# The MLP of the first eight tiles moved into the second batch pair's attention, and the stretch behind it put in a modelled order

## The chip, the cores and the metric

The kernel runs on one core of one Trainium2 chip, in one launch. A core has five engines that are programmed apart: TensorE (PE; its weight loads are listed apart as PEld), VectorE (DVE), ScalarE (ACT), GpSimd (POOL) and SyncE (SP), the last of which here only issues DMAs. Each engine runs its own queue of instructions in order and waits on semaphores for the others. The metric is the time of one execution on the device in microseconds (us), and less is better.

## What is computed

Input is x with B, T, C = 4, 1024, 128 in float32, and the output has the same shape. Four blocks follow one another, each on the layer norm of what came before:

```python
x = x + attention(layernorm(x))     # 16 heads of 8; a row sees its last 32 rows and every 64th one before it
x = x + ffn(layernorm(x))           # h = [x, -x]; weights +1 or -1
x = x + mamba(layernorm(x))
x = x + ffn(layernorm(x))           # the same weights

def ffn(x):                                          # k0 256x512, k1 512x512, k2 512x128: bool
    h = s0 * (concat([x, -x]) @ where(k0, 1., -1.))
    h = s1 * ((relu(h) * 2) @ where(k1, 1., -1.))
    return s2 * ((relu(h) * 2) @ where(k2, 1., -1.))

def mamba(x):                                        # E = 256 channels, N = 16 states
    u, z = split(layernorm_gb(x) @ W_in)             # 128 -> 2 x 256
    u2 = silu(conv4(u) + conv_b)                     # depthwise, causal, 4 taps
    dt_lo, Bm, Cm = split(u2 @ W_xp)
    dt = softplus(dt_lo @ W_dt + b_dt)
    h[t] = exp(dt[t] * A) * h[t-1] + dt[t] * u2[t] * Bm[t]   # per channel and state
    y = (sum over states of h * Cm) + u2 * D_param
    return x + res_scale * ((y * silu(z)) @ W_out)
```

## The kernel before

All work on the four compute engines is issued through a thin wrapper (`InOrder`, L49 to L60). While the list `keep` is not empty, each instruction is pinned to its place in program order, so that within its engine nothing overtakes; where the list is empty, the build's scheduler may move instructions by its own priorities. Since the call that records every instruction is L57, nearly all rows of the profile have that line, and the tiles' names tell them apart.

**Data.** The rows are held in two buffers `xs[0]` and `xs[1]`, one for each pair of batches (bp). A tile is 128 rows: 64 of each batch of the pair. A pair has 16 tiles, and a chunk (bp, c) is four tiles, 512 columns once turned. The notation "(0,2)" below is chunk 2 of pair 0. For Mamba a part (b, f) is one half (f) of one batch (b).

**Stage 1, attention (L201 to about L591).** A software pipeline of turns, one tile each: 32 tiles, with seven turns ahead (`LEAD`, L541) and five behind. In turn i the stages of several tiles are issued one after the other, in the order that is written out in the loop (L546 on): POOL's `strided_products` of tile i-1 (prodv) and `product` of i+1 (prod); PE's `weights` of i-2 (pt, four transposes); on DVE `scores_before`, `divide` of i-4, `strided` of i-2 (or), `weights_own` (eo); ACT copies pt into ep and POOL subtracts eo from it (`weights_before`); PE's output projection of i-5 (py) and DVE's residual; PE's `scores` of i+1 (ps), which ACT copies into S; DVE's `softmax_scores` (the strided sums, the row maximum mx, the subtraction) and ACT's two exponentials (E); PE's `turn_out` (po) and `values` (pa). Each tile of a pair has one more strided row block than the one before, so prod, prodv, or and S grow within a pair. Between these stages two steps of `prep_steps` (L274 to L349) of a later chunk are issued: the normalised rows xn, their transposes tp and xnT, the projections pq, pk and pn, the loads that spread the keys into kx (L330) and the values into vd, vr (L342, L345). `spread_values` (L477) copies vr into the value blocks on ACT, one quarter a turn in turns 4c-1 to 4c+2 of its chunk. PSUM has eight banks of 2 KB for each partition: ps has two, mx one, and five in turn serve all else (`spare`, L213). `stats` and `scales` (L244, L254) make the norm's factors (sta and mva on DVE, rsa on POOL). At turn 0 SP loads the MLP's weights as bytes (`load_mlp`, L106).

**Between attention and scans (L648 to L1237).** DVE turns the bytes into float32 weights w0, w1 and w2, in buffers that a pool frees again (L648 to L675). Mamba's weights are loaded on SP and POOL's queues (L792 to L835), among them `taps`, 512 KB, from which w_conv is made. The MLP (`mlp`, L682) takes one chunk: statistics (st_f, mv_f, rs_f), normalised rows (fxn), transposes (ftp, fxnT), the first layer (pf to h1), the second (pg to h2: 64 matmuls of 512 columns for a chunk, in two groups of 32), the third (pfo), and the residual. Each activation is held as a high and a low half in a format called f32r, so w0 and w1 are applied twice, while w2 is applied in float32. Names have an a behind them for the first MLP and b or c for the one at the end (pga, pgb, pgc). In the first batch pair's case the statistics (L244's kind, in the trace st_fa, mv_fa, rs_fa) are placed by the scheduler as soon as rows are ready.

Such a function is a generator of `Piece`s: a few instructions with a rough cost for each engine and the PSUM banks that they take. A `Work` (L598 to L645) is a stream of them. Two lanes of work hold the MLP chunks: lane 0 has (0,0), (0,2), (1,0), (1,2) of the first MLP, then chunks of the last one; lane 1 the odd ones. For the first scan part two more works run beside them: `mamba_norm` (L848: statistics, factors rs_z, rows mxn, transposes, the norm that becomes x itself, mxnT) of chunks (0,0) and (0,1), and `mamba_pre_half` (L903: pc, the four taps as matmuls; px; pd; dt; du). The loop at L1216 to L1237 gives each of the works one piece in turn, but the lanes none while `mamba_pre_half` has a PE piece next, until du of the first part is there. `keep` is empty here.

**Scans (L1044).** 128 units, one for each of 8 parts and 16 states: db (POOL), da (ACT), the scan hs (DVE), pcc (PE), hc (DVE), their sum (POOL) and pys (PE). Within a unit, `evictions` and `pieces` (L1155, L1165) issue pieces of the other works, by budgets for each engine (`RATES`, L1144) and three spare banks (`SPARE`, L1142). `ready` (L1185) forces what a part needs. At the end of the scans what is left of the works is issued, and then (L1255 on) the last batch's output (pmo_own) and its MLP (pfc, pgc, pfoc).

Of the kernel before, what the change touches and what calls it, by code (L numbers as in the profile page):

```python
# [16 lines left out]
F32 = mybir.dt.float32  # L17
BF16 = mybir.dt.bfloat16
I32 = mybir.dt.int32
U8 = mybir.dt.uint8  # L20
# [6 lines left out]
P = 128  # L27
# [16 lines left out]
def hybrid_kernel(ctx: ExitStack, tc: tile.TileContext, x, Wq, Wk, Wv, Wo, ln_g, ln_b, W_in, conv_w,  # L44
# [56 lines left out]
    k0s = const.tile([P, 2, FF], U8, name="k0s")  # L101
    k1s = const.tile([P, 4, FF], U8, name="k1s")
    k2s = const.tile([P, 4, C], U8, name="k2s")
    scal = const.tile([P, 4], F32, name="scal")

    def load_mlp():  # L106
        for t, k in ((k0s, k0), (k1s, k1), (k2s, k2)):
            nc.sync.dma_start(t, k.rearrange("(i p) f -> p i f", p=P))
        for i, s in enumerate((s0, s1, s2, res_scale)):
            nc.sync.dma_start(scal[:, i : i + 1], s.partition_broadcast(P))  # L110
# [88 lines left out]


    def attention(actx):  # L201
# [8 lines left out]
        pr = actx.enter_context(tc.tile_pool(name="attpr", bufs=5, space=PSUM))  # L210
# [63 lines left out]
        def prep_steps(cc):  # L274
# [3 lines left out]
            xn = ap2.tile([P, 4, C], F32, name=f"xn{cc}", tag="xn")  # L278
# [11 lines left out]
            xnT = ap2.tile([P, CH], F32, name=f"xnT{cc}", tag="xnT")  # L290
# [33 lines left out]
            else:  # L324
                kT = ap2.tile([P, CH], F32, name=f"kT{cc}", tag="kT")
# [17 lines left out]
            vr = ap2.tile([P, 16, C], F32, name=f"vr{cc}", tag="vr")  # L343
# [7 lines left out]
        S, E, prods, prodv, ew, psum, outs = ({} for _ in range(7))  # L351
# [54 lines left out]
        def softmax_scores(i):  # L406
# [9 lines left out]
            mx = pw.tile([P, H], F32, name=f"mx{i}", tag="mx")  # L416
# [119 lines left out]
        def residual(i):  # L536
            bp, m = tiles[i]
            ve.tensor_add(xs[bp][:, m, :], xs[bp][:, m, :], psum.pop(("y", i))[:, :C])
# [3 lines left out]

        starts = {(3 if cc == 1 else 4 * cc) - LEAD: cc for cc in range(len(tiles) // 4)}
        preps = []
        last = len(tiles)
        for i in range(-LEAD, last + 5):  # L546
# [6 lines left out]
            if i == 0:  # L553
                load_mlp()
# [14 lines left out]
            if i >= 0:  # L569
                at(1, scores)  # L570
                at(1, keep_scores)
            at(0, softmax_scores)
            at(0, softmax_exp)
# [5 lines left out]
            at(-3, values)  # L579
            at(-4, keep_out)  # L580
# [7 lines left out]
            cc, step = divmod(i + 1, 4)  # L588
            if 0 <= cc < last // 4:
                spread_values(cc, range(step, step + 1))  # L590
# [57 lines left out]
    fw = ctx.enter_context(tc.tile_pool(name="ffnw", bufs=1))  # L648
    fx = ctx.enter_context(tc.tile_pool(name="ffnx", bufs=2))
    with tc.tile_pool(name="kload", bufs=1) as kl:  # L650


        sign = fw.tile([P, 2], F32, name="sign")
        below = fw.tile([P, 2], F32, name="below")
        ve.tensor_single_scalar(sign, scal[:, 0:2], 0.0, op=ALU.is_gt)
        ve.tensor_single_scalar(below, scal[:, 0:2], 0.0, op=ALU.is_lt)
        ve.tensor_sub(sign, sign, below)
        total = fw.tile([P, 1], F32, name="total")
        ve.tensor_mul(below, scal[:, 0:2], sign)
        ve.tensor_scalar_mul(below, below, 2.0)  # L660
        ve.tensor_mul(total, below[:, 0:1], below[:, 1:2])
        ve.tensor_mul(total, total, scal[:, 2:3])
        twice = fw.tile([P, 2], F32, name="twice")
        ve.tensor_scalar_mul(twice, sign, 2.0)

        w0 = fw.tile([P, FF], F32R, name="w0")
        diff = kl.tile([P, FF], F32, name="diff")
        ve.tensor_sub(diff, k0s[:, 0], k0s[:, 1])
        ve.tensor_scalar_mul(w0, diff, twice[:, 0:1])
        w1 = fw.tile([P, 4, FF], F32R, name="w1")  # L670
        ve.tensor_scalar(w1, k1s, twice[:, 1:2], sign[:, 1:2], ALU.mult, ALU.subtract)
        w2 = fw.tile([P, 4, C], F32R, name="w2")
        ve.tensor_scalar(w2, k2s, 2.0, -1.0, ALU.mult, ALU.add)
    waste = fw.tile([P, C], F32, name="waste")
    fed = set()  # L675
# [121 lines left out]
    def vec(name, src, n):  # L797
        t = mw.tile([P, n], F32, name=name)
        nc.gpsimd.dma_start(t, src.rearrange("(h p) -> p h", p=P))
        return t  # L800

    g_t, b_t = vec("ln_g", ln_g, 1), vec("ln_b", ln_b, 1)
    cb_t, bdt_t, dp_t = vec("cb", conv_b, NH), vec("bdt", b_dt, NH), vec("dp", D_param, NH)
    w_in = mw.tile([P, 2 * E], F32, name="w_in")
    nc.sync.dma_start(w_in, W_in)

    w_xp = mw.tile([P, NH, 6 * N + DR], F32, name="w_xp")
    xp = W_xp.rearrange("(h p) r -> p h r", p=P)
    for i in range(3):
        nc.gpsimd.dma_start(w_xp[:, :, 2 * N * i : 2 * N * (i + 1)], xp[:, :, DR:])  # L810
    nc.gpsimd.dma_start(w_xp[:, :, 6 * N :], xp[:, :, :DR])
    w_dt = mw.tile([6 * N + DR, E], F32, name="w_dt")
    nc.gpsimd.dma_start(w_dt[6 * N :, :], W_dt)
    a_t = mw.tile([P, NH, N], F32, name="a_t")
    nc.gpsimd.dma_start(a_t, A_log.rearrange("(h p) n -> p h n", p=P))
    sc.activation(a_t, a_t, AF.Exp)
    ve.tensor_scalar_mul(a_t, a_t, -1.0)
    w_out = mw.tile([P, NH, C], F32, name="w_out")
    nc.sync.dma_start(w_out, W_out.rearrange("(h p) c -> p h c", p=P))
    gp.tensor_scalar_mul(w_out, w_out, scal[:, 3:4])  # L820

    w_conv = mw.tile([P, DC, E], F32, name="w_conv")
# [375 lines left out]
    def in_scan_buffers(u):  # L1198

        return [m2.tile([P, 2, CH], F32R, name=f"h1{u}_{f}", tag="hc", bufs=6) for f in range(4)]  # L1200
# [89 lines left out]
```

## Time and profile before

| | |
|---|---|
| median of 3 runs | 929.82 us (927.71 to 930.09) |
| profiled execution, its own time | 926.49 us |
| span of the profiled execution | 924.7 us |
| PE busy | 759.3 us (82%), 5642 matmuls |
| DVE busy | 756.4 us (82%), 1013 instructions |
| ACT busy | 592.4 us (64%), 1299 instructions |
| POOL busy | 747.9 us (81%), 586 instructions |
| mean granted clock of PE | 0.896 of full |
| DMA | 53.09 MB, mean 57 GB/s |
| chain that ended last | DVE 30%, PE 26%, POOL 17%, ACT 14%, issue 8% |
| 0 to 136.6 us: busy PE, DVE, ACT, POOL | 100.43, 113.45, 75.59, 116.77 us |
| 240.1 to 248.5 us: busy PE; clock | 5.05 us; 0.58 |

The profile is of one execution. Busy is the sum of the durations of an engine's instructions; the chain follows the last instruction back to what released it, step by step. A stretch is given as start and end from the span's start. A row "out<-in" names the tile that an instruction writes and those that it reads; "<-POOL prodv" behind an idle time names what ended it.

### The profile page before, as it was taken

The page shows a single profiled execution, that of the slowest core. Times are in us where ns is not written, and L with a number is a line of the kernel's source. Part 1 is how long each engine was busy: PE and PEld are TensorE (multiplying, and loading weights), DVE is VectorE, ACT ScalarE, POOL GpSimd, SP SyncE. Part 2 cuts the span into 40 slices and gives each one's busy share as a digit, 9 for nine tenths or more (in the row PEclk, how much of TensorE's full clock was granted, in tenths as well). Part 3 has the DMA queues.
Part 4 walks back from the last instruction along what each step waited for, and adds up shares of the span by engine and source line. Part 5 has one row for each costly group of instructions (what it writes and reads, how often), then busy time and mean ns, then how long its engine had stood idle before and what let it go on. Part 6 is the DMA issues. An engine that isn't in the chain of part 4 may idle for free.

```text
span 924.7 us, 15264 instructions
## 1 busy us (share of the span) xinstructions
PE 759.3 (82%) x5642; PEld 455.5 (49%) x5642; DVE 756.4 (82%) x1013; ACT 592.4 (64%) x1299; POOL 747.9 (81%) x586
## 2 busy tenths in 40 slices
PE   5797768865788979897789798869889798888887
PEld 2455435543466534542356444425446355554566
DVE  6699898999633278889799888898998999999842
ACT  4775537743345577889867767876878765655413
POOL 6699996999533188999989988999989999989621
PEclk9899769997599979897999989968989899898998
DMA  4633123330100111121111122121121212121000
GB/s 122 128 71 70 41 37 68 73 65 2 42 7 1 47 69 50 45 67 70 68 58 58 46 68 71 45 70 46 69 82 62 86 50 78 69 80 58 24 23 12
DMA packets 47162, 53.09 MB, mean 57 GB/s; under 512 B 4824, under 2 KB 38400, under 8 KB 47088
## 3 DMA queue, kind: packets, MB, share of 16 engines
q1 hardware_dynamic: 45920, 51.59, 19.7%
q8 instruction: 44, 0.72, 0.3%
q0 software_dynamic: 608, 0.27, 0.2%
q10 hardware_dynamic: 560, 0.26, 0.1%
q14 instruction: 30, 0.25, 0.1%
HBM read 45.82 MB, written 4.46 MB: 54 GB/s over the span
## 4 chain that ended last, share of the span: by engine, by line
DVE 30%; PE 26%; POOL 17%; ACT 14%; issue 8%; SPq 3%; DMA 1%; DVEq 0%; POOLq 0%; ACTq 0%
DVE hs L57 14%; DVE hc L57 4%; PE pga L57 4%; PE pys L57 4%; POOL db L57 4%; POOL prod L57 3%; DVE S L57 3%; ACT da L57 3%; POOL prodv L57 3%; PE pgb L57 2%; PE pc L57 2%; SPq L330 2%; ACT L57 2%; POOL hc L57 2%; PE pfoa L57 2%
## 5 line engine op out<-in xcount | busy, mean ns | idle before, releaser
L57 POOL TENSOR_TENSOR db<-du,bs 128x1024 f32<-128x1024 f32 x128 | 302.5, 2364 | 0.4 <-DMA bs<-bd 0.4
L57 ACT ACTIVATE da<-dt,a_t 128x512 f32<-128x512 f32 x256 | 175.4, 687 | 126.7 <-DVE hs L57 126.3
L57 POOL TENSOR_TENSOR hc<-hc,hc 128x512 f32<-128x512 f32 x128 | 163.0, 1274 | 43.7 <-DVE hc L57 43.6
L57 DVE TENSOR_TENSOR hc<-hs,pcc 128x1024 f32<-128x1024 f32 x128 | 156.0, 1219 | 28.6 <-PE pcc L57 21.1
L57 DVE TENSOR_TENSOR_SCAN hs<-da,db 128x512 f32<-128x512 f32 x128 | 149.4, 1207 | 14.3 <-ACT da L57 14.1
L57 DVE TENSOR_TENSOR_SCAN hs<-da,carry,db 128x512 f32<-128x512 f32 x128 | 157.1, 1267 | 4.5 <-ACT da L57 4.5
L57 PE MATMUL pys<-hc,ident 128*128 128x512 f32 x256 | 146.0, 655 | 0.8 <-POOL hc L57 0.8
L57 PE MATMUL pcc<-bc,spread 96*128 96x512 bf16 x128 | 52.8, 413 | 34.8 <-DVE hc L57 33.8
L57 PE MATMUL pga<-h1a,w 128*128 128x512 f32 x256 | 73.9, 439 | 3.1 <-ACT gate L57 2.2
L57 PEld LDWEIGHTS pys<-hc,ident 128*128 128x128 f32 x256 | 51.0, 209 | 51.2 <-issue 31.8
L57 POOL TENSOR_TENSOR prodv<-vS,E 128x128 f32<-128x128 f32 (+14 forms) x30 | 69.3, 2311 | 5.8 <-ACT E L57 5.6
L57 POOL TENSOR_TENSOR prod<-kv,qs 128x128 f32<-128x128 f32 (+14 forms) x30 | 71.1, 2369 | 1.5 <-DVE or L57 1.4
L57 PE MATMUL pc<-mxnT,w_conv 128*128 128x512 f32 x128 | 61.7, 608 | 5.9 <-ACT gate L57 5.9
L57 PEld LDWEIGHTS pga<-h1a,w 128*128 128x128 f32 x256 | 51.2, 202 | 27.6 <-issue 7.3
L57 ACT ACT_TABLE_LOAD x48 | 61.6, 1283 | 3.4 <-issue 2.6
L57 PE MATMUL pgb<-h1b,w 128*128 128x512 f32 x192 | 58.9, 453 | 4.4 <-DVE fxnTc L57 3.1
L57 ACT ACTIVATE E<-S 128x512 f32<-128x512 f32 (+15 forms) x62 | 26.5, 473 | 52.3 <-DVE S L57 52.1
L57 PE MATMUL ps<-kx,qT 64*32 64x256 f32 x1008 | 47.8, 448 | 6.3 <-DVE S L57 5.4
L57 PEld LDWEIGHTS pgb<-h1b,w 128*128 128x128 f32 x192 | 38.0, 199 | 26.7 <-issue 7.8
L57 PE MATMUL py<-woT,oT 128*128 128x128 f32 x64 | 18.0, 368 | 40.0 <-ACT oT L57 39.8
L57 POOL TENSOR_TENSOR ep<-ep,eo 128x512 f32<-128x512 f32 x32 | 40.9, 1278 | 9.9 <-ACT ep L57 8.7
L57 ACT COPY ep<-pt 128x512 f32<-128x512 f32 x32 | 18.7, 586 | 38.4 <-DVE eo L57 36.5
(217 smaller groups left out, 1560.9 us busy)
## 6 DMA issues: line engine op xcount, KB each, us to landing
bs<-bd SPq DMA_DIRECT2D x64, 512.0 KB
vr<-vd SPq DMA_DIRECT2D x32, 256.0 KB
vd<-kv SPq DMA_DIRECT2D x8, 256.0 KB
x<-in_L_attn_a_x_dram SPq DMA_DIRECT2D x15, 128.0 KB
kx<-kT SPq DMA_DIRECT2D x104, 16.0 KB
out_dram<-x SPq DMA_DIRECT2D x12, 128.0 KB
taps<-in_L_attn_b_conv_w_dram SPq DMA_DIRECT2D x1, 512.0 KB
k1s<-in_L_ffn_k_dram SPq DMA_DIRECT2D x1, 256.0 KB
```

Source lines behind the costliest of these rows:

```text
L57: ins = getattr(self.engine, name)(*args, **kwargs)
L330: queues[h % len(queues)].dma_start(kx[rows, :, h % HB, :], kT[rows, :].rearrange("p (t x) -> p t x", t=4))
```

## The change

1. **Weights and loads.** The MLP's bytes have no buffers of their own any more. At turn 15 they are loaded into the attention buffer of pair 0's keys and values (tag "kv"), which is free then, and turns 16 to 19 make w0, w2 and w1 of them on DVE. Mamba's loads (`load_mamba`, now 11 on SP and none on POOL) are issued at turn 8; taps, w_dt and w_out come after the attention. w_conv, spread, minus_i and the scaling of w_out are pieces of a work of their own (`tables_between`).
2. **MLP of tiles 0 to 7.** It runs in the second pair's turns (17 to 33), in pairs of tiles, 256 columns: `first_te` issues one of four PE steps a turn (transposes and the third layer of the pair before; 8 matmuls of the first layer; two steps of 16 of the second), `first_sc` and `first_ve` empty its banks one turn later. Statistics stand in turns 15 and 16, and those of the following norm in turns 33 and 34. The lanes begin with (0,2) and (0,3), and `mamba_norm` takes the ready factors.
3. **PSUM.** Six banks in place of five serve the attention's `spare`; mx has none of its own, and is put into columns 128 to 143 of the bank that py of five tiles before has used.
4. **Other buffers.** xn, xnT, kT and vr have one buffer in place of two. The loads of vr are issued two turns later, `spread_values` copies two quarters a turn in turns 4c+1 and 4c+2, and chunk 1's preparation starts a turn later.
5. **Order between attention and scans.** It is pinned, and made by a small model: each engine has a time from which it is free, each work one from which its next piece can start, and the piece with the earliest start is next; lanes get a malus of 1.0 us, and may hold at most five banks together with the others.

The diff, cut to its core:

```diff
-    def load_mlp():
-        for t, k in ((k0s, k0), (k1s, k1), (k2s, k2)):
-            nc.sync.dma_start(t, k.rearrange("(i p) f -> p i f", p=P))
+    def load_scales():
...
+    def mlp_weights(k0s, k1s, k2s):
...
+        ve.tensor_scalar_mul(twice, sign, 2.0)
+        yield
+        ve.tensor_sub(w0, k0s[:, 0], k0s[:, 1])
+        ve.tensor_scalar_mul(w0, w0.bitcast(F32), twice[:, 0:1])
+        ve.tensor_scalar(w2, k2s, 2.0, -1.0, ALU.mult, ALU.add)
+        for i in range(2):
+            yield
+            part = slice(2 * i, 2 * i + 2)
+            ve.tensor_scalar(w1[:, part], k1s[:, part], twice[:, 1:2], sign[:, 1:2], ALU.mult, ALU.subtract)
...
-        pr = actx.enter_context(tc.tile_pool(name="attpr", bufs=5, space=PSUM))
+        pr = actx.enter_context(tc.tile_pool(name="attpr", bufs=6, space=PSUM))
...
-            mx = pw.tile([P, H], F32, name=f"mx{i}", tag="mx")
+            mx = (left_over.pop(i) if i in left_over else spare(f"mx{i}"))[:, C : C + H]
...
-            ve.tensor_add(xs[bp][:, m, :], xs[bp][:, m, :], psum.pop(("y", i))[:, :C])
+            left_over[i + 5] = py = psum.pop(("y", i))
+            ve.tensor_add(xs[bp][:, m, :], xs[bp][:, m, :], py[:, :C])
...
+        def first_te(k):
+            p, step = divmod(k, 4)
+            h1, xnT, h2, xn = (first[n] for n in ("h1", "xnT", "h2", "xn"))
+            if step == 0:
+                if p:
+                    po = first["po"] = spare(f"mo{k}")[:, :cols]
+                    for t in range(2):
+                        for f in range(4):
+                            te.matmul(
+                                po[:, t * C : (t + 1) * C], h2[:, f, t * C : (t + 1) * C], w2[:, f].bitcast(F32),
+                                start=f == 0, stop=f == 3,
+                            )
+                if 2 * p < FIRST:
+                    tp = first["tp"] = spare(f"mt{k}")[:, :cols]
+                    for t in range(2):
+                        te.transpose(tp[:, t * C : (t + 1) * C], xn[:, t * C : (t + 1) * C], ident)
+            elif step == 1:
...
+                            te.matmul(
+                                pf[:, f], w0[:, (f0 + f) * P : (f0 + f + 1) * P], xnT[:, s], start=s == 0, stop=s == 1
+                            )
+            else:
+                f0 = 2 * step - 4
+                pg = first["pg"] = spare(f"mg{k}").rearrange("p (f c) -> p f c", f=2)
+                for f in range(2):
+                    for j in range(4):
+                        for s in range(2):
+                            te.matmul(
+                                pg[:, f], w1[:, j, (f0 + f) * P : (f0 + f + 1) * P], h1[:, j, s],
+                                start=j + s == 0, stop=j == 3 and s == 1,
+                            )
...
+            if i == NT // 2:
+                load_mamba()
+            if i == NT - 2:
+                finish_mamba()
+            if i == NT - 1:
+                first_rooms()
+                weights_made = mlp_weights(*first["codes"])
+            step = i - NT - 1
+            if step == 0:
+                first_norm(0)
+            if 0 < step <= STEPS:
+                first_sc(step - 1)
             at(-1, strided_products)
...
             if i >= 0:
                 at(1, scores)
                 at(1, keep_scores)
+            if 0 < step <= STEPS:
+                first_ve(step - 1)
+            if NT <= i < NT + 4:
+                next(weights_made, None)
             at(0, softmax_scores)
+            if NT - 1 <= i <= NT:
+                first_stats(range(4 * (i - NT + 1), 4 * (i - NT + 2)), "mv")
+            c = i - NT - STEPS
+            if 0 <= c < 2:
+                first_stats(range(4 * c, 4 * c + 4), "after")
             at(0, softmax_exp)
...
             at(-3, values)
+            if 0 <= step < STEPS:
+                first_te(step)
             at(-4, keep_out)
...
-            early(0, lane, f1, lane, *[in_scan_buffers] * lane),
             early(0, 2 + lane, f1, lane),
...
-            wanted = first[-1].may() and "pe" in first[-1].next.us
-            for w in first + ([] if wanted else lanes):
-                if w.may():
-                    w.run()
+            able = []
+            for w in first + lanes:
+                if not w.may() or (w in lanes and w.next.banks and w.held + w.next.banks + sum(v.held for v in first) > 5):
+                    blocked.add(w)
+                    continue
...
+                start = max([since[w], *(free[k] for k in w.next.us)])
+                able.append((start + (1.0 if w in lanes else 0.0), len(able), start, w))
+            start, w = min(able)[2:]
+            us = w.next.us
+            w.run()
+            end = start + sum(us.values()) + (0.1 if us else 0.0)
+            since[w] = end
+            for k in us:
+                free[k] = end
```

## The prediction, made before the changed kernel ran

> **What bounds the kernel now.** I read four views of the profile, in this order. First the busy time by stage, with stage borders that I took from the timeline: 136.6 us is where the second batch's first turn starts, 240.1 the end of its last full turn, 248.5 the last residual of the attention, 324.6 the first scan (hs), 885.9 the end of the last one. The columns are the stage, its length, busy time of PE, PEld, DVE, ACT and POOL, the granted clock of PE, the DMA share and GB/s.
>
> ```profile
> 136.60:187.10 50.50, 45.63 (x971) 29.41 (x969) 46.39 (x101) 37.30 (x99) 41.69 (x39) 0.98 0.34 67
> 187.10:240.10 53.00, 31.73 (x777) 22.24 (x776) 49.48 (x71) 19.18 (x46) 53.00 (x21) 0.77 0.15 29
> 248.50:324.60 76.10, 67.48 (x294) 48.39 (x295) 27.62 (x68) 43.03 (x86) 22.27 (x34) 0.91 0.10 29
> 324.60:885.90 561.30, 478.92 (x1700) 267.01 (x1699) 506.64 (x493) 406.56 (x845) 507.44 (x373) 0.91 0.18 61
> 885.90:924.70 38.80, 30.04 (x207) 25.82 (x205) 8.69 (x24) 9.17 (x24) 5.12 (x10) 0.90 0.07 21
> ```
>
> The second batch's attention runs DVE and POOL full (POOL 53.00 of 53.00 in its second half), while PE has room (31.73 of 53.00) and a low clock, 0.77. The 76.1 us between attention and scans are the reverse: PE 67.5, DVE 27.6, POOL 22.3. So two stages with opposite bounds lie one after the other.
>
> Second, the chain of work that ended last, in order of time, between attention and scans (start, us, what):
>
> ```profile
> 261.33 15.25 PE pga L57 x64
> 276.58 5.37 PE pfoa L57 x48
> ...
> 285.26 1.88 POOL rs_z L57 x2
> ...
> 295.25 5.35 PE pga L57 x23
> 300.61 6.87 PE pc L57 x16
> ...
> 311.98 1.72 PE px L57 x4
> ...
> 324.58 2.35 DVE hs L57 x2
> ```
>
> From 248.5 to 287.4 it is the MLP of chunks (0,0) and (0,1), eight tiles, with the statistics of the norm after it; then the norm, in which pga of chunk (0,2) stands ahead of pc; from 300.6 on the preparation of the first scan part: pc, px, pd, dt, du, db, hs.
>
> Third, the timeline of the first batch at 105 us, for the statistics that are there today:
>
> ```profile
> 105.62 1.04 POOL L57 TENSOR_TENSOR rs_fa<-rs_fa,minus_half 128x4 f32<-128x4 f32 x1
> ...
> 112.40 1.75 DVE L57 TENSOR_REDUCE or<-prodv 128x128 f32<-128x1536 f32 x1 [3.09 <-POOL prodv L57]
> ```
>
> VectorE sat idle 3.09 us for a POOL product that stood behind rs_fa and rsa. The later MLP's statistics (16 pairs st_fa and mv_fa, 0.28 + 0.17 us each, and four rs_fa groups of 1.77 us) are already in the attention, between 52 and 163 us.
>
> Fourth, the chain at the end:
>
> ```profile
> 889.59 3.57 PE pfoc L57 x32
> 893.16 1.80 PE pfob L57 x16
> ...
> 895.79 4.12 PE pmo_own L57 x32
> ```
>
> The last batch's output waits until PE has emptied the lanes (pfob), so work that the lanes still owe after the last scan comes straight onto the end.
>
> **What the Trainium skill says.** "Perfetto Trace Analysis", Optimization Strategy: where the most-contended engine changes over time, interleaving the regimes may help. The first two views show such a pair. "TensorE: Matmul & The Clock Gate", What's actually happening: PE's default clock is the throttled one and activity releases it. The stage table agrees in direction: 0.98 where PE is busy 45.6 of 50.5, 0.77 where 31.7 of 53. Same page, LDWEIGHTS and Back-to-back issue gap: a load of 128 columns takes 128/1.2 = 107 ns, a warm matmul of 256 columns 109 ns. This trace has pairs with 128 columns of f32 at 7.30 us for 64 records (pfoa), 0.114 each, and 512-column f32r at 15.43 us for 64 (pga), 0.241 each; the 256-column f32r of the change is not in it.
>
> **The change part by part.** Sums are against the profiled execution, 926.49 us with a span of 924.7; the median of the runs is 929.82, 0.36% above it. I carry the difference over to the median.
>
> (1) Between attention and scans. Gone: MLP of (0,0) and (0,1), their statistics, the weights, most of the loads. The order of the changed build puts the two norms first, then pc. From the end T of the attention: ACT in order mxn 1.65, x 1.65, mxnT 0.78, mxn 1.65, fxn of (0,2) 1.65, x 1.65, mxnT 0.78 = 9.8 us (four times 0.41 a group, and the mxnT row). The factors rs_z come from POOL during the drain. taps is issued at T and w_conv in the old trace ran 254.88 to 256.85, 8.4 us after T, so the taps load is hidden under ACT by 1.4 us; if it were not, it costs its excess. Then pc 6.9, pfa 0.9 and ftpa 0.6 ahead of px, and from px to hs 12.6 as before (311.98 to 324.58). Sum 9.8 + 6.9 + 1.5 + 12.6 = 30.8, against 76.1: **-45**. Bounds: -41 if the other lane's fxn and pfa collide, -48 if the copy of dtl (it waited 1.6 us for h1a) now comes at once.
>
> (2) Second batch. PE gets per pair of tiles 2 transposes (0.25), 8 + 32 f32r matmuls of 256 columns and 8 of f32 (16 records, 1.8). Per f32r matmul at least 0.11 (0.114 above), at most 0.241; I take 0.13, since load and stream overlap in both rows. Pair: 0.25 + 40 x 0.13 + 1.8 = 7.3; four pairs 29 us over 17 turns, 1.7 a turn (2.1 at most in one). The turns of the old timeline, from one mx to the next, have 4.7 to 5.8 us of PE in 5 to 6 us (turns 18 to 24, sum 39.4), and 3.9 to 5.2 in 6.7 to 9 later. Base without preparation is 3.3 (ps 1.1, pa 1.0, pt 0.7, py 0.4, po 0.1), preparation 0.9 to 1.7. With the steps: 5.1, 6.9, 6.6, 6.8, 5.1, 6.9, 6.6 for turns 18 to 24. DVE gets per pair 0.41 + 0.43 + 2 x 0.68 = 2.2 (rows fxnTa, x, h1a, the first two scaled to half), the weights 0.68 + 0.49 + 0.42 + 1.4 + 8 x 0.16 = 4.3, and 16 pairs of statistics at 0.45; 16 old ones leave. In turns 18 to 24 that makes 5.1, 6.2, 4.4, 5.0, 6.2, 7.0, 6.0. ACT gets 3.6 a pair, to some 5.6 a turn. Taking the largest engine of each turn (and the old 6.1 in turn 18, which waited on ACT) gives 45.7: **+6**. Turns 15, 16, 17: statistics 1.8 in each of the first two less 0.45, small weight operations 1.3 in turn 16, w0 and w2 in turn 17: +1.4, +1.9, +1.1, all on DVE: **+4**. Turns 25 to 31: DVE +4.1, but DVE had 3.0 us idle behind POOL in turns 30 and 31, so **+2**. The drain: 3.6 of statistics and the last PE steps, beside engines that are mostly idle; **+2**, between -1 (a warm PE: the drain ran at 0.58) and +5.
> New wait: mx now lies in the bank of py, so pt of the next turn, at the head of PE's queue with py, ps and values behind it, waits for DVE's subtraction. eo, which needs pt, stands 2.5 us into DVE's turn and pt takes 0.7, so I count nothing; uncovered it would be at most 0.7 a turn, 12 us. ACT's eviction of a step stands ahead of ep and the scores' copy, with POOL's ep behind: likewise nothing, up to 0.6 a turn.
>
> (3) First batch. Leaving: 8 pairs of statistics on DVE (3.6 us) and two rs_fa on POOL (3.5) in turns where these engines are full; they run side by side, so about 4; the spread copies no longer hold ACT behind a load in turns 0 to 3: 1. **-5**, between 0 and -9. The MLP codes, and Mamba's loads (11 on SP, some 0.5 us of issue each), go into SP's idle time at 15.8 to 23.5 and after the vd of chunk 4; POOL loses 11 issues at 251 to 260, hidden before.
>
> (4) Scans. Before the first scan the old build has chunk (0,2) done and (0,3) in pga; the new has pfa of (0,2). So 48 f32r matmuls, pfa and pfoa, some 16 us of PE, move into the scans. The order of the build shows that lag kept to the end: there 48 matmuls, pfb, ftp, pfc and half of pfob stand behind the last unit, which did not before. The scans issue as much as before: **0**, from -5 to +10 (the second part's preparation is now at unit 28, need at 30).
>
> (5) The end. Behind the last scan come, beyond the old, 48 x 0.241 = 11.6, pfb and pfc (3.8), ftpb and ftpc (1.1), half of pfob 1.8, nothing else for DVE or POOL to do, and one more handover of h1 (about 1.3) : **+19**, from 15 to 24.
>
> Sum: -45 + 6 + 4 + 2 + 2 - 5 + 0 + 19 = **-17**. I take 4 us off for handovers between three engines at 6 to 7 us a turn, which a largest-engine sum leaves out: **-13**, 913.5 us for the profiled execution, **916.8** for the median.
>
> **The rivals.** A, PE becomes the attention's bound (slower). If 256 columns cost the full 0.241, steps total 4 x (0.25 + 9.6 + 1.8) = 47 us. In turns that are already at 90% PE, and in the in-order queue behind a late ep, all of it would show. Then -45 + 47 + 4 - 5 + 19 = +20: 950. It decides for slower from 26 us of growth in the attention (45 - 19). For it: PE 45.6 of 50.5. Against it: 64 pairs with loads ran at 0.114, and half the steps fall in turns with 3 us of room. B, the steps hide altogether, helped by the clock: no growth in attention beyond the 4 of DVE, -45 + 4 - 5 + 19 = -27: 903. For it: the clock 0.77, ACT 19 of 53. C, the lag is paid twice: the scans grow 10 by late preparation on top of the forecast, -3: 927, no difference. For it: part (0,1) is prepared two units before it is needed, against seven or eight; against it: the budget of pieces is the same.
>
> **How the numbers follow.** Forecast 0.46, B 0.20, C 0.14, A 0.20 (a part of A stops short of 950). About 0.3% (2.8 us) is what a measurement of this kernel can tell from no change. Faster: 0.46 + 0.20 + a third of C and a little of A, 0.72; same 0.10; slower 0.18. The forecast's own range is 908 to 925; for 8 in 10 it goes from 900, just below B, to 938, into A.
>
> **What would show it.** Right: the gap from the last py to the first hs near 31 us; turns 18 to 24 sum to 44 to 48 us; clock in 187 to 240 above 0.85; the scans 556 to 571 us; the tail from the last hs near 58 us. Wrong: a mean step matmul above 0.2 us apart, DVE idle behind ps or eo in turns 18 to 25 (A), or hs waiting for du or bs at unit 32 (C).

## The result and the profile after

| | before | changed |
|---|---|---|
| median of 18 runs each | 927.32 us (924.44 to 930.39) | 931.15 us (928.42 to 934.07) |
| profiled execution, own span | 924.7 us | 929.0 us |

The ratio is 1.0036, with a 95% interval of 1.0022 to 1.0050: the changed kernel is slower by a third of a per cent. The prediction said faster, -13 us in the profiled execution; its span grew by 4.3. So 17 us have to be found. (The prediction started from the median of three runs, 929.82 us; the 18 runs give 927.32, and the comparison is by ratio.)

The stage table of the changed kernel (columns as in the prediction: stage, length, busy PE, PEld, DVE, ACT, POOL, clock, DMA share, GB/s). The rows are turns 16 to 24, turn 25 to the end of the last full turn, the stretch between attention and scans, the scans, and the rest:

```profile
142.40:207.90 65.50, 57.16 (x1062) 40.72 (x1055) 55.19 (x111) 42.08 (x112) 40.56 (x34) 0.95 0.27 50
207.90:264.70 56.80, 44.92 (x864) 37.35 (x862) 54.30 (x79) 25.89 (x61) 53.59 (x21) 0.82 0.13 27
272.50:308.10 35.60, 24.43 (x51) 11.02 (x52) 13.16 (x29) 23.34 (x45) 15.08 (x20) 0.64 0.14 49
308.10:865.30 557.20, 473.12 (x1696) 264.71 (x1695) 504.13 (x488) 407.80 (x859) 510.35 (x379) 0.92 0.18 62
865.30:929.00 63.70, 52.34 (x301) 41.77 (x300) 15.01 (x34) 18.25 (x40) 5.06 (x10) 0.90 0.05 13
```

The stretch between attention and scans has indeed gone from 76.1 to 35.6 us. The second batch and the tail moved up: 65.5 + 56.8 where the batch had 50.5 + 53.0, and 63.7 behind the scans where there were 38.8. The scans are 4.1 us shorter.

The lengths of all stages, worked out from each trace, in us. A turn begins here with the reduction that gives the row maximum of its tile, so what the loop issues in turn i ahead of that reduction lies in row i-1; "drain" goes from turn 31's to the last residual, "between" from there to the first hs, and the border between scans and tail lies 1.5 us behind the end of the last hs (885.9 in the kernel before, as in the prediction). The start is no part of any comparison: in the kernel before and in e6, which differ in the scans alone, it took 47.0 and 44.2 us.

| kernel | to turn 4 | 4-14 | 15 | 16-17 | 18-24 | 25-30 | drain | between | scans | tail |
|---|---|---|---|---|---|---|---|---|---|---|
| before | 47.0 | 80.6 | 9.0 | 11.1 | 39.4 | 44.0 | 17.4 | 76.1 | 561.3 | 38.8 |
| changed | 48.6 | 80.9 | 12.9 | 18.1 | 47.5 | 47.7 | 16.8 | 35.6 | 557.2 | 63.7 |
| e1_evict_later | 46.7 | 80.9 | 12.9 | 14.8 | 47.4 | 46.9 | 19.1 | 34.7 | 556.9 | 63.0 |
| e2_rate | 47.1 | 80.9 | 12.9 | 18.1 | 47.5 | 47.8 | 16.7 | 36.1 | 577.0 | 33.7 |
| e3_high_only | 48.5 | 81.0 | 12.8 | 17.7 | 46.1 | 47.8 | 16.8 | 34.9 | 559.4 | 63.9 |
| e4_no_steps | 47.0 | 80.8 | 12.9 | 15.8 | 39.4 | 44.0 | 18.3 | 36.8 | 558.3 | 64.0 |
| e5_a_t_later | 49.0 | 76.6 | 13.0 | 18.1 | 47.8 | 47.7 | 16.8 | 35.8 | 557.5 | 63.8 |
| e6_before_rate | 44.2 | 80.6 | 9.0 | 10.3 | 39.4 | 44.0 | 17.0 | 77.8 | 578.6 | 35.0 |
| e7_norm_first | 49.4 | 80.8 | 12.9 | 18.1 | 47.5 | 47.8 | 16.7 | 31.0 | 551.0 | 67.0 |
| e8_own_first | 49.0 | 80.8 | 12.9 | 18.1 | 47.2 | 47.7 | 17.3 | 36.5 | 572.6 | 42.4 |
| e9_all | 46.9 | 76.8 | 10.7 | 13.2 | 48.5 | 46.9 | 19.1 | 30.4 | 589.8 | 34.5 |
| e10_attention | 46.2 | 76.6 | 10.7 | 13.3 | 48.5 | 46.9 | 19.0 | 30.3 | 553.3 | 64.8 |
| e11_rate_34 | 46.7 | 76.7 | 10.7 | 13.9 | 48.4 | 46.8 | 18.8 | 30.3 | 576.5 | 40.3 |

Three places in the changed trace stand out. First, VectorE in the loop's turn 14, in the first batch (timeline: start, length, engine, line, operation, tiles, count, and in brackets the idle time before it with what ended it):

```profile
114.22 1.08 DVE L57 TENSOR_SCALAR a_t<-a_t 128x32 f32<-128x32 f32 x1 [4.84 <-ACT a_t L57]
...
116.36 1.74 DVE L57 TENSOR_REDUCE or<-prodv 128x128 f32<-128x1536 f32 x1
```

and ScalarE just before:

```profile
111.19 1.66 ACT L57 ACTIVATE xn<-x,rsa 128x128 f32<-128x128 f32 x4
112.72 1.23 ACT L57 COPY vb<-vr 32x512 f32<-32x512 f32 x2
113.96 0.23 ACT L57 ACTIVATE a_t<-a_t 128x32 f32<-128x32 f32 x1
```

The change puts the preparation of Mamba's table a_t into turn 14: an exponential on ScalarE, then a sign on VectorE. In the kernel before both come after the attention (260.93 and 261.19 us). ScalarE comes to it only behind xn and two vb copies, and VectorE, which takes its queue in order, waits 4.84 us with the whole turn behind the waiting instruction.

Second, row 17 (the loop's turn 18): VectorE waits for ScalarE's high half of xnT, with the strided sums and the row maximum behind it:

```profile
159.03 0.42 DVE L57 TENSOR_TENSOR xnTm<-mt,xnTm 128x256 fp32r<-128x256 f32 x1 [3.34 <-ACT xnTm L57]
```

Third, the chain between attention and scans, and the chain at the end (start, us, what):

```profile
276.37 2.89 POOL rs_fa L57
...
284.98 9.36 PE pc L57 x16
...
308.07 2.35 DVE hs L57 x2
```

```profile
874.74 7.46 PE pgc L57 x32
...
888.67 7.48 PE pgb L57 x32
...
900.86 4.12 PE pmo_own L57 x32
```

A factor of the lanes' MLP (rs_fa) stands in the chain to the first scan, where the prediction had only the two norms, and pc took 9.36 us where the kernel before needed 6.87; the granted clock was 0.76 while pc ran (285.0 to 294.3 us), against 1.00 before (300.6 to 307.5). Behind the last scan, TensorE does two whole second layers before it may begin with the last batch's output. (A chunk's second layer has 32 matmuls, in two groups of 16, and not 64 as the description of the kernel says.)

### The profile page after: what moved, and what is told of

Read it like the earlier page. It is cut to its first block, busy times and chain, and to the rows that moved or that the text cites. A ratio compares the mean times of both kernels' runs of the same rounds, so it can differ in the third digit from the quotient of the medians.

```text
span 929.0 us, 15444 instructions
## 1 busy us (share of the span) xinstructions
PE 760.9 (82%) x5722; PEld 460.1 (50%) x5722; DVE 764.8 (82%) x1010; ACT 595.3 (64%) x1317; POOL 744.7 (80%) x573
## 3 DMA queue, kind: packets, MB, share of 16 engines
q1 hardware_dynamic: 48400, 51.73, 19.8%
## 4 chain that ended last, share of the span: by engine, by line
DVE 35%; PE 28%; POOL 17%; ACT 14%; issue 6%; DMA 1%; POOLq 0%; DVEq 0%; ACTq 0%
DVE hs L57 11%; DVE S L57 7%; POOL db L57 6%; PE pc L57 4%; PE pys L57 4%; POOL hc L57 4%; DVE or L57 3%; DVE hc L57 3%; ACT da L57 3%; ACT L57 3%; PE pga L57 2%; DVE py L57 2%; PE pgb L57 2%; POOL rs_z L57 2%; PE pgc L57 2%
## 5 line engine op out<-in xcount | busy, mean ns | idle before, releaser
L57 DVE TENSOR_TENSOR hc<-hs,pcc 128x1024 f32<-128x1024 f32 x128 | 156.0, 1219 | 30.3 <-PE pcc L57 22.8
L57 POOL TENSOR_TENSOR prodv<-vS,E 128x128 f32<-128x128 f32 (+14 forms) x30 | 69.4, 2315 | 19.8 <-ACT E L57 9.9
L57 PE MATMUL pgb<-h1b,w 128*128 128x512 f32 x192 | 56.4, 444 | 5.0 <-ACT gate L57 3.3
L57 PE MATMUL ps<-kx,qT 64*32 64x256 f32 x1008 | 47.8, 453 | 15.3 <-DVE S L57 12.7
L57 PE MATMUL pga<-h1a,w 128*128 128x512 f32 x192 | 56.9, 444 | 1.1 <-ACT gate L57 1.0
L57 PEld LDWEIGHTS pga<-h1a,w 128*128 128x128 f32 x192 | 38.5, 204 | 20.4 <-issue 8.4
L57 PEld LDWEIGHTS pc<-mxnT,w_conv 128*128 128x128 f32 x128 | 25.0, 196 | 31.6 <-issue 30.0
```

Of the source, the lines that this page charges most:

```text
L57: ins = getattr(self.engine, name)(*args, **kwargs)
```

## The experiments

My theory after reading the trace: the parts that leave were sized rightly, and most of the missing 17 us are new waits and operations in VectorE's queue, plus one in ScalarE's. The rivals: TensorE bounds the attention (rival A of the prediction), or the lag of the lanes is what costs, and is avoidable.

**Evictions of the steps later (e1).** VectorE's part of a step goes behind the softmax's subtraction.

```diff
-            if 0 < step <= STEPS:
-                first_ve(step - 1)
             at(0, softmax_scores)
...
             at(0, softmax_exp)
+            if 0 < step <= STEPS:
+                first_ve(step - 1)
```

> VectorE's share of a step (the low halves xnTm and h1m, the residual of mo) is issued behind the subtraction of the row maximum and not ahead of the strided sums. Handover theory: in the changed kernel VectorE stood still 5.2 us before xnTm and 1.7 us before h1m, waiting for ScalarE, with the whole turn's softmax behind it; those waits now lie beside the exponentials, turns 16 to 31 go from 122.3 us to about 117, the time by -5 us against the changed kernel (about 926). Rival, TensorE bounds these turns: the idle time reappears before eo, and the time falls by 1 us or less.

In this kernel the statistics of tiles 6 and 7 are read ahead of their last residual (in turn 34), which changes the values but no place that is read here. Ratio to the kernel before 1.0006 (0.9989 to 1.0023), median 927.95 us: 2.8 us below the changed kernel by the ratio, where I had expected 5. Turns 16 and 17 fell by 3.3 us; turns 18 to 24 by nothing (47.4 for 47.5), turns 25 to 30 by 0.8, and the drain grew by 2.3. VectorE goes from the residual straight on to the strided sums (S) of turn 18:

```profile
153.50 0.28 DVE L57 TENSOR_TENSOR x<-x,py 128x128 f32<-128x128 f32 x1
153.70 1.15 DVE L57 TENSOR_SCALAR w<-codes,twice,sign 128x1024 fp32r<-128x1024 uint8 x1
154.76 0.40 DVE L57 TENSOR_REDUCE S<-prod 128x32 f32<-128x256 f32 x1
```

So the handover cost the one wait of 3.34 us. In turns 18 to 24 the rival was right: there VectorE's waits for pt ahead of eo grew from 2.5 us in two places to 4.5 in five, and 17% of the chain that ended last were the steps' second layer (mg). The idle time moved and the turns stayed as long.

**Half of the matmuls (e3) and no steps at all (e4).**

```diff
-                        for s in range(2):
-                            te.matmul(
-                                pg[:, f], w1[:, j, ...], h1[:, j, s],
-                                start=j + s == 0, stop=j == 3 and s == 1,
-                            )
+                        te.matmul(pg[:, f], w1[:, j, ...], h1[:, j, 0], start=j == 0, stop=j == 3)
```

(e3 does the same to pf; e4 removes the calls of first_norm, first_te, first_sc and first_ve.)

> The first two layers of the moved MLP leave out the low half of the activations, so its steps have 4 and 8 matmuls in place of 8 and 16 (outputs differ); evictions stay. That takes 4 x 20 x 0.13 = 10.4 us from TensorE in turns 17 to 32. TensorE theory: turns 16 to 31 shrink by 4 us or more, from 122.3 to 118 or less, most of it in turns 19 to 25. Handover rival: they shrink by 1.5 us or less, since VectorE still waits for ScalarE's evictions.

> The MLP of tiles 0 to 7 is left out altogether (outputs differ); its weights, its statistics, the six banks, the shared mx, the single buffers and the two spread copies a turn stay. Theory that the steps cost the attention what it grew by: turns 16 to 31 come down from 122.3 us to about 109 (the 103.5 of before, 4.4 us of statistics and weights on VectorE, 1 us of two spread copies). Rival, the rest of the change (shared bank, spread copies, chunk loads later) costs it: they stay above 114. In the first 16 turns nothing may change (turn 16 at 142.4 us).

e3: one run of 930.73 us, span 928.9. Some 10 us of matmuls less on TensorE bring turns 16 to 30 from 113.3 to 111.6, 1.7 us: close to the 1.5 of the handover theory, far from 4. So rival A does not hold as it was priced, and VectorE's waits were still there in e3. Whether TensorE and these waits limit turns 18 to 24 by turns, so that taking away either alone shows little, is open: no run takes away both. e4: one run of 919.05 us, span 917.3. Turns 18 to 24 and 25 to 30 take 39.4 and 44.0, the figures of the kernel before: the shared bank of mx, six banks, single buffers and two spread copies a turn cost nothing there without the steps. So it is the steps that make these turns longer. Turns 18 to 24 and 25 to 30, first of the kernel before, then of the changed one (columns as above):

```profile
147.70:187.10 39.40, 35.98 (x762) 23.08 (x754) 36.04 (x76) 30.04 (x77) 33.75 (x26) 1.00 0.41 80
187.10:231.10 44.00, 26.01 (x665) 17.81 (x665) 42.65 (x60) 17.34 (x41) 44.00 (x18) 0.81 0.18 34
```

```profile
160.50:208.00 47.50, 44.31 (x774) 32.41 (x773) 40.86 (x79) 32.01 (x82) 31.82 (x21) 0.96 0.34 61
208.00:255.70 47.70, 37.97 (x764) 31.00 (x763) 46.49 (x68) 22.86 (x54) 46.63 (x18) 0.82 0.15 32
```

In the second stretch VectorE is as full as before, with a single wait of 0.60 us, and its 3.8 us of added work match the 3.7 us of growth. In the first stretch the growth is 8.1 us; VectorE's work grew by 4.8 and it has gaps, and TensorE is busy 93% of the time.

With turn 31, which takes 9.0 in both, turns 16 to 31 of e4 come to 108.2 us, where I had expected 109. Turns 15 to 17 stay long without the steps. Windows of turn 15 and of turns 16 and 17, first of the kernel before, then of the changed one, then of e4:

```profile
127.60:136.60 9.00, 4.71 (x69) 2.61 (x56) 8.86 (x16) 2.56 (x7) 8.37 (x4) 0.76 0.06 11
136.60:147.70 11.10, 9.65 (x217) 6.33 (x215) 10.35 (x26) 7.26 (x23) 7.94 (x14) 0.89 0.09 18
```

```profile
129.50:142.40 12.90, 8.07 (x129) 4.79 (x131) 12.41 (x31) 3.14 (x7) 5.73 (x3) 0.75 0.35 53
142.40:160.50 18.10, 12.96 (x292) 8.40 (x284) 14.38 (x34) 10.17 (x30) 8.84 (x14) 0.90 0.08 21
```

```profile
127.80:140.70 12.90, 8.45 (x182) 5.31 (x180) 12.41 (x30) 3.14 (x7) 5.75 (x3) 0.87 0.36 55
140.70:156.50 15.80, 8.66 (x145) 5.05 (x145) 15.38 (x34) 6.56 (x23) 8.02 (x13) 0.84 0.06 13
```

The third number of busy times is VectorE: 12.41 of 12.90 and 15.38 of 15.80 in e4. There the three turns take 28.7 us against 20.1 before, and VectorE's busy time grew by the same 8.6 us: eight pairs of statistics (3.6, and 1.3 of old ones left), the small sign operations (2.4), w0, w2 and half of w1 (4.3); these durations overlap a little at their ends. A full engine shows all of it. One operation is longer in e4 than in the changed kernel: w2 takes 1.49 us for 0.41, beside a POOL instruction (149.74 to 151.19).

**The table's sign moved (e5).**

```diff
         sc.activation(a_t, a_t, AF.Exp)
-        ve.tensor_scalar_mul(a_t, a_t, -1.0)
...
         ve.tensor_scalar_mul(minus_i, ident[: 4 * N, : 4 * N], -1.0)
+        ve.tensor_scalar_mul(a_t, a_t, -1.0)
```

> One small VectorE operation (the sign of Mamba's table a_t) is moved from turn 14 to the stretch after the attention; ScalarE's exponential stays. Theory: my forecast of -5 us for the first batch was right in what leaves, and this operation took it back, since VectorE waited 4.84 us for ScalarE's exponential, which stands behind four xn and two vb copies. Then turn 13 to 16 takes 31 us in place of 35.3, and the time falls by 3 to 4 us, to about 927.5. Rival: POOL, which was busy without a gap from 104.8 to 129.3 us, sets these turns and hides VectorE's wait; the three turns stay at 35 and the time within 1 us.

Ratio 0.9999 (0.9984 to 1.0014), median 926.88 us: 3.4 us below the changed kernel by the ratio, as expected. Turns 4 to 14 fell from 80.9 to 76.6, 4.3 us; turns 13 to 15 alone from 35.3 to 31.1. Here VectorE goes from o to the sums or without a gap:

```profile
110.60 0.29 DVE L57 TENSOR_TENSOR o<-pa,rden 128x128 f32<-128x128 f32 x1
110.80 1.74 DVE L57 TENSOR_REDUCE or<-prodv 128x128 f32<-128x1536 f32 x1
```

The rival, that POOL hides the wait, is wrong: POOL was full up to 129.3 us, but then stood still for 3.2 us before prodv of tile 15 (132.52 us): this needs the exponentials of tile 15 (131.44), and these VectorE's subtraction (130.47), which came late; in e5 that prodv follows ep without a gap, at 129.62.

**Norm ahead of the lanes (e7).**

```diff
         since[first[2]] = 5.0
+        since.update((w, 9.0) for w in lanes)
```

> In the modelled order between attention and scans the lanes may begin only 9 us in, so both chunks of the norm go ahead of the lanes' statistics, rows and transposes. Theory: ScalarE waited 3.4 us for the lane's factors rs_fa in front of the second chunk's x and mxnT, and that wait goes; from the last residual of the attention to the first scan 32 us in place of 35.6. Rival: the taps' load and w_conv, or POOL behind VectorE's two long table operations, come last there, and it stays at 35 or more.

One run of 924.01 us, span 922.2; between takes 31.0 in place of 35.6. The rows of ScalarE, first of the changed kernel, then of e7:

```profile
281.03 1.65 ACT L57 ACTIVATE fxna<-x,rs_fa 128x128 f32<-128x128 f32 x4 [3.38 <-POOL rs_fa L57]
282.58 1.63 ACT L57 ACTIVATE x<-x,rs_z 128x128 f32<-128x128 f32 x4
```

```profile
278.30 1.64 ACT L57 ACTIVATE x<-x,rs_z 128x128 f32<-128x128 f32 x4
279.84 0.77 ACT L57 ACTIVATE mxnT<-mtp,ln_b,ln_g 128x512 f32<-128x512 f32 x1
285.44 1.65 ACT L57 ACTIVATE fxna<-x,rs_fa 128x128 f32<-128x128 f32 x4 [4.83 <-POOL rs_fa L57]
```

The wait for rs_fa is still there, and even longer. It no longer stands ahead of pc, which begins 7.5 us after the last residual in place of 12.5 and runs beside it. But it still stands ahead of u, which the first scan needs, and the chain of e7 goes through it:

```profile
287.86 1.25 ACT fxna L57 x3
289.12 1.28 ACT L57
290.42 0.69 ACT u L57
291.11 0.04 issue
291.15 1.98 PE px L57 x4
```

The row without a tile is a load of ScalarE's function table. In e7 px begins 1.9 us after the end of pc (289.25), in the changed kernel 1.4 (294.34 to 295.70).

**The budget in the scans (e2, e6) and the order of the tail (e8).**

```diff
-    RATES = {"pe": 2.9, "ve": 1.2, "sc": 2.4, "gp": 1.2}
+    RATES = {"pe": 3.8, "ve": 1.2, "sc": 2.4, "gp": 1.2}
```

(e2 does this to the changed kernel, e6 to the kernel before; e8 changes two things at once: it has 3.3, and puts the last batch's output, statistics and norm first in the list of works that is emptied behind the scans, with some of their tiles in other buffers.)

```diff
+        finals = [Work(late_batch(B - 1, range(2 * k, 2 * k + 2), None, k, own)) for k in range(2)]
+        works[:0] = [Work(mamba_out_own(B - 1)), *finals]
         while any(...):
             evictions()
             pieces(forced=True)
```

> Only the budget of TensorE pieces within a scan unit is raised, from 2.9 to 3.8 us. Lag theory: the work that the two lanes still owed after the last scan (pfc, pgc, pfoc, pfb, pgb, pfob, some 31 us of the 63.7 us tail) is done within the scans, where TensorE was busy 3.70 us of 4.35 a unit; by the slope over units of the changed trace (0.3 us of unit for 1 us of pieces) the scans grow from 557 to about 567: the time falls by some 20 us, to about 911. Rival, the scans are as much bound by TensorE as by the others: what leaves the tail comes back in the scans, the time stays within 3 us of the changed kernel's 931.

> The kernel before, with the budget of TensorE pieces at 3.8 us a unit in place of 2.9. Lag theory: before, the lanes owed only pgc (16), pfoc and half of pfob at the last scan, some 9 us, part of it beside the last scan's own chain, so there is little to bring forward and the scans are stretched as they were in the changed kernel (19.8 us for 29.8): the time goes from 927 to 925 to 930, and the budget belongs to the change. Rival: the budget was too small before as well, and the kernel before gains 7 us or more; then the change is no better than the budget.

> Budget 3.3 us a unit, and the last batch's output (pmo_own), its statistics and its norm are issued ahead of what the lanes still owe after the last scan, so that the lanes' matmuls (half of pgc, pfoc and half of pfob, 9 us) run while the statistics and the norm of the last batch are made; TensorE stood idle there for 5.4 us. By the stage sums: scans 568 us (18 us moved into them at 0.66 each), tail about 39 us in place of 63.7, time 14 us below the changed kernel's, about 917. If the lag were not what makes the tail, the tail would stay above 50.

e2: ratio 0.9936 (0.9913 to 0.9960), median 919.54 us, 9 us below the changed kernel by the ratio. The tail fell by 30.0 us as expected, but the scans grew by 19.8, twice what I had taken from the slope: -10 and not -20. e6: ratio 1.0133 (1.0099 to 1.0167), median 938.30 us: tail -3.8, scans +17.3. I had expected no change within 3 us; neither theory had it. In these two pairs the larger budget stretched the scans by much the same (17.3 and 19.8 us), though there was little to bring forward in the one and much in the other. e8: ratio 0.9973 (0.9959 to 0.9988), median 924.06 us, which is 6 us below the changed kernel by the ratio where I had expected 14: tail -21.3 (I had said 39 us, it is 42.4), scans +15.4. With the last batch first, TensorE's longest gap behind the scans is 2.48 us, where e2 has 3.71 between the last batch's output and its MLP. What the lanes still owed there, 11.4 us of matmuls (16 of pgc, pfoc, half of pfob), stands between these two, and the tail is 8.7 us longer than in e2.

**All together (e9, e10, e11).** The edits of e5, e7 and e1 (with the last residual left ahead of the statistics), the small sign operations in turn 0, the second operation of w0 and all of w1 on ScalarE, with three budgets: 3.8 (e9), 2.9 (e10), 3.4 (e11).

```diff
+            if i == 0:
+                signs = mlp_signs()
...
-        ve.tensor_scalar_mul(w0, w0.bitcast(F32), twice[:, 0:1])
+        sc.activation(w0, w0.bitcast(F32), AF.Identity, scale=twice[:, 0:1])
...
-            ve.tensor_scalar(w1[:, part], k1s[:, part], twice[:, 1:2], sign[:, 1:2], ALU.mult, ALU.subtract)
+            sc.activation(w1[:, part], k1s[:, part], AF.Identity, bias=minus[:, 1:2], scale=twice[:, 1:2])
```

> All edits together: table sign after the attention, VectorE's part of a step behind the subtraction (the residual of the last step still ahead of the statistics), the small sign operations in turn 0, the second operation of w0 and all of w1 on ScalarE, lanes from 9 us on, and the budget 3.8. If the places found are separate, their gains add: turns 13 to 15 -4.3, turn 15 -2.3 (small operations), turns 16 to 18 -3.3 and -2, between -4.6, and -10 by the budget: 26 us below the changed kernel, about 904 where the kernel before has 927. If they hide one another, it stays above 910.

> The same without the budget (2.9 as in the changed kernel). By the stage sums 16 to 17 us below the changed kernel's 931: about 914; scans 550 to 556 us and a tail of some 64 to 68, since the lanes' lag is still paid at the end. With the run beside it this gives the worth of the budget on the mended order; if that is below 5 us, the lag was no separate cause.

> The same with the budget 3.4, at which half of pgc, pfoc and half of pfob (9 us) are left after the last scan, as in the kernel before. From the other two budgets: of each us taken out of the tail 0.66 came back in the scans, so the time lies between the two, some 3 us above that of 3.8 (about 907); if the scans stretch more than in proportion near 3.8, it is the same or faster.

| kernel | budget | median | ratio to the kernel before | scans + tail |
|---|---|---|---|---|
| e10_attention | 2.9 | 915.31 us | 0.9866 (0.9842 to 0.9889) | 618.1 us |
| e11_rate_34 | 3.4 | 911.56 us | 0.9835 (0.9808 to 0.9862) | 616.8 us |
| e9_all | 3.8 | 918.41 us | 0.9905 (0.9887 to 0.9924) | 624.3 us |

e10 came out as expected (914): against the changed kernel, the gains of turns 4 to 14 (-4.3), 15 (-2.2), 16 and 17 (-4.8) and between (-5.3) add, and turns 18 to 30 and the drain take 2.4 back. e9 did not: 904 expected, and 918.41 lies above the 910 from which I had said that the gains hide one another. From e10 to e9 the scans grew by 36.5 us, and the tail fell by 30.3. e11, for which I had expected 907, or the time of e9 or less, is the fastest of all, and by 1.65% faster than the kernel before. Its scans and tail:

```profile
292.30:868.80 576.50, 497.80 (x1790) 282.98 (x1788) 511.78 (x500) 418.19 (x876) 510.29 (x379) 0.89 0.17 60
868.80:909.10 40.30, 31.70 (x212) 27.11 (x210) 8.68 (x24) 9.46 (x25) 5.17 (x10) 0.87 0.07 20
```

With the mended order the budget is worth 3.7 us at best (915.31 to 911.56; the two intervals of the ratio overlap), less than the 5 from which I had called the lag a separate cause. TensorE's pieces can be put into the scans or into the tail, and the sum of both stayed within 617 to 624 us in these three; in e2 it was 610.7. For each us that left the tail, the scans grew by 0.66 in e2, 0.95 in e11 and 1.20 in e9.

## Why the prediction failed, step by step

Four steps failed. Step (3) left out an operation that the change puts into the first batch, and its wait: 5.3 us. Step (2) priced VectorE's additions in turns 15 to 17 too low, and put the wait for xnTm nowhere: 6.9 us. Step (1) left out the wait for rs_fa and took too little for pc: 4.5 us. Step (5) took 5.9 us too little for the end, of which the scans gave 4.1 back. In the profiled execution, forecast and measured:

| step | forecast | measured |
|---|---|---|
| (1) between | -45 | -40.5 |
| (2) turns 15 to 17 | +4 | +10.9 |
| (2) turns 18 to 30 | +6 and +2 | +8.1 and +3.7 |
| (2) drain | +2 | -0.6 |
| (3) first batch: turns 4 to 14; start | -5 | +0.3; +1.6 |
| (4) scans | 0 | -4.1 |
| (5) the end | +19 | +24.9 |
| handovers, not placed | +4 | in the rows above |
| sum | -13 | +4.3 |

**Step (3) failed by omission.** "Leaving: 8 pairs of statistics ... and two rs_fa" was right: with a_t out of turn 14 (e5), turns 4 to 14 are 4.0 us shorter than in the kernel before. But I counted what leaves and not what the same diff puts in: finish_mamba's sign on VectorE, an instruction of 1.08 us with 4.84 of waiting. Moving it alone gave 4.3 us.

**Step (2), turns 15 to 17: mis-sized.** My own prices for these turns (statistics 1.35 twice, small operations 1.3, w0 and w2 1.6) add up to 5.6 us, and I wrote 4.4 and took 4, without a reason. Idle time could not have hidden more than 0.9: before, VectorE was busy 8.86 of 9.00 us in turn 15 and 10.35 of 11.10 in turns 16 and 17. And the prices were low: e4 measured 8.6 us, where the small operations took 2.4, w0's second operation 1.01 for the 0.49 that I had read, and half of w1 fell into row 17. The changed kernel has 2.3 us more than e4. The wait for xnTm is 3.34, and e1 got 3.3 back by moving VectorE's part; w2, longer by 1.1 in e4, hides the difference. I had a row for handovers, but put such a wait nowhere.

**Step (2), turns 18 to 30:** +11.8 for +8. The largest engines of turns 18 to 24, as listed, add up to 46.2 and not to 45.7 us; the sum was near, but what fills these seven turns is not shown, as said at e3.

**Step (1): right in mechanism, short by 4.5.** "fxn of (0,2)" was in my row of ScalarE's work at 1.65 us, without the wait for its factors, 3.38: pc began 12.5 us after the last residual, where I had 9.8. The rest is pc itself, 9.36 us for 6.9. From pc's end to the first scan it took 13.7 us, where I had 14.1. e7 finds the 31 us that the prediction named, but in other parts, and that is luck: pc begins at 7.5, and takes 8.54.

**Steps (4) and (5): together +20.8 for +19.** The 64-record rows were good prices (pgc 7.46 us for 32 matmuls, 0.233 each). The tail alone was 6 us longer than forecast, and the scans were 4 us shorter. In the tail the two lanes run one after the other, each with its own pfc or pfb, 32 matmuls of the second layer and 32 of the third; how the 6 us divide was not measured. That work moves and does not vanish was right: before, TensorE was busy 67.5 of the 76.1 us that were cut to 35.6, and part of that was the lanes' next chunks. That a larger budget would have won 20 us back was my expectation for e2, and was wrong: the sum of scans and tail fell by 10 us there, and by 1.3 at the best on the mended order. Why the same 3.8 gave scans of 577.0 us on one order and 589.8 on the other is open.

**The matmul price** (0.13 us at 256 columns) held at the full clock: five of the eight steps of 16 took 2.16 to 2.18 us. The other three, in turns where the clock was 0.63 to 0.83, took 2.56 to 3.25. Rival A, which put the loss on TensorE at 0.241 us a matmul, named the right sign with a wrong price.

Of the prediction's own signs, turns 18 to 24 (47.5 us, within 44 to 48) and the scans (557.2) came true; the gap (35.6 for 31), the clock of the second half (0.82 for above 0.85) and the tail from the last hs (65.2 for 58) did not.

With the waits mended, e10's ratio is 0.9866; the prediction's 916.8 to 929.82 is 0.9860. That they meet so closely is in part chance: e10 also takes work off VectorE that the forecast had left there, turns 18 to 30 (+12.0) and the tail (+26.0) stay above the forecast, and the scans (-8.0) below it. It is no proof of each term. The separate runs show 4.3 us (e5), 3.3 (e1, whose drain takes 2.3 back) and 4.6 (e7, one run) of the 17.

## What to carry to other kernels

When work is moved into a stage whose engines take their queues in order, list every instruction that comes with it, the tiny ones too, and ask of each what it waits for and what stands behind it; an operation of 0.2 us that waits for another engine's last item of the turn can cost that engine's whole delay (4.3 us here). On VectorE, busy 98% of turn 15, an addition cost its full length. And before a stretch is cut, subtract from the gain the useful work that went on beside it, for it will be paid later.

## What the runs showed of the hardware

Two small VectorE operations ended only with the POOL instruction beside them. VectorE and POOL in turn 15 of the changed kernel, and the same VectorE operation in turn 0 of e10:

```profile
140.73 1.27 DVE L57 TENSOR_SCALAR below<-below 128x2 f32<-128x2 f32 x1
```

```profile
140.71 1.26 POOL L57 TENSOR_TENSOR ep<-ep,eo 128x512 f32<-128x512 f32 x1 [3.73 <-ACT ep L57]
```

```profile
24.94 0.24 DVE L57 TENSOR_SCALAR below<-below 128x2 f32<-128x2 f32 x1
```

The sign of a_t took 1.08 us beside an ep that ran from 114.01 to 115.26, and 0.16 after the attention in e5; POOL's power for rs_fa took 2.89 us while VectorE made w_conv (276.36 to 278.36), and 1.04 for the second one. The Trainium skill's page "SBUF — State Buffer", section "Who interferes with whom", says that VectorE and GpSimd share a pair of ports, that tensor_scalar can take it in some modes and a tensor_tensor with two inputs in SBUF contends for it too, and that the one that issues second blocks for the whole instruction. These rows agree, in both orders: the ep instructions began first, and w_conv began first. No run here tried it by itself.
